# Cross-attention on one core: probabilities loaded back a slot later, keys stored in three planes

## The chip, the cores and the metric

The kernel runs on one core of a Trainium2 chip, alone. The metric is the time of one execution on the device in microseconds; the median of several runs counts. The engines are TensorE (PE, its weight loads shown as PEld), VectorE (DVE), ScalarE (ACT), GpSimd (POOL) and SyncE (SP), which here only issues DMAs.

## The reference

The input x is [32, 512, 640] float32, the context [32, 77, 1024], the weights are [640, 640] for queries and output and [1024, 640] for keys and values. There are 20 heads of 32 columns. The other slices of the context (objects, others, image prompt) are empty, so that one attention is left:

```
q = heads(x @ wq);  k = heads(ctx @ wk);  v = heads(ctx @ wv)     # 20 heads of 32
p = softmax(q k^T / sqrt(32))                                     # 512 x 77 per head
out = merge(p v) @ wo + bo + x
```

All products are made from float32 numbers split into a high and a low part: a product is three matmuls, high by high, high by low and low by high (`PAIRS`).

## The kernel before, in words

**Layout.** The 640 columns are five chunks j of 128 columns, four heads each. A *slot* n is one batch b and one chunk j (n = 5b + j, 160 slots). The keys and values of all 2464 context rows (five groups g of 512 rows, the last of 416) are computed in a prologue, split, and stored to scratch in HBM (`k_dram`, `v_dram`). The main loop loads them back per batch.

**Prologue.** For each group, `keys` and `values_of` make the products on TensorE, `split_keys` splits a key tile into high and low in a `ks` tile (two buffers) and issues its stores: three DMAs per tile, by GpSimd for all groups but the last, by SyncE for the last. The value products of the last group (`context_values(LAST, j, psv)`) are left for later: two before slot 0, one in slot 0 and two in slot 1 (`beside`).

**A slot.** In slot n TensorE makes the scores of chunk n in four parts (`scores`, L477), the queries of chunk n+1 in two parts (`queries`, L442), the attention values of an earlier chunk (`values`, L569), and two *pieces* of an output projection (`piece`, `project`, L612) of an earlier batch. ScalarE does the exponentials (`exps`, L495); GpSimd normalizes the chunk before (`normalize`, L510). `transpose_p(n - 1)` then transposes 32 x 32 blocks on DVE (z, L517) and stores the probabilities to HBM with four DMAs (pd, L524). `load_p` reads them back in another layout with two DMAs (raw, L533 and L534). A slot later the chunk is *taken*: `cast_p` (ACT, pp, L541), `rest_p` (ACT L547 and DVE L548) and `last_p` (POOL, L555) split it, `values` multiplies it, `sum_a`, `high_a` and `low_a` (L580 to L594) make the tile `at` that the projection reads.

**Lags.** `LAG = 3`: slot n takes chunk n-3, whose load was issued in slot n-1. Seen from the slot that loads: slot n calls `load_p(n - LAG + 1)`, which is chunk n-2, and the store of chunk n-2 stands late in slot n-1 (`transpose_p`). The ten pieces of a batch's projection are spread over the slots by `PIECES[j]` (batches back, first piece), the residual loads (xr, L601) and bias additions (POOL, L605) by `RESIDUAL` and `BIAS`.

**Output banks.** A projection half of 128 rows accumulates in one of two PSUM tiles `po`. `finish()` adds a completed half to its residual row block on DVE (L641), which frees the bank, and stores the rows (L647). Where `finish()` is called decides where that addition stands in DVE's order.

**Keys and values per batch.** Chunks 0 and 1 form group 0, chunks 2 to 4 group 1 (`GROUPS`). For each group there are two key tiles: `kb`, with the 308 columns of four heads for the high part of the query, and `kc`, with two halves of 154 columns for the other two products. `load_keys` issues two DMAs per head (L420, L423); `load_values` issues eight DMAs per group (L431). `refill` calls them in two halves per slot.

**Order.** The order of every engine is the order in which the program calls it; each engine runs its own list in order and waits on semaphores. SyncE issues all the DMAs of the main loop. A DMA on it also waits until the one issued eight before it has landed, since the completion semaphores are eight (DMAHW0 to DMAHW7) and are used in turn.

Of the kernel before, what the change touches and what calls it, by code (L numbers as in the profile page):

```python
# [51 lines left out]
def kernel(  # L52
# [41 lines left out]

    k_dram = dram.tile([P, NC_, 2, NT], FPR, name="k_dram")

    v_dram = dram.tile([NT + KPAD - NKEY, HPC, NC_, 3, HD], FPR, name="v_dram")
    wo_dram = dram.tile([P, NC_, 2, C], FPR, name="wo_dram")  # L100
# [106 lines left out]
    def split_keys(g, j):  # L207
        g0, gn = GROUPS_KV[g]
        ks = kvt.tile([P, 2, G], FPR, tag="ks", name="ks")
        split(ks[:, 0, :gn], ks[:, 1, :gn], pks.pop(j)[:, :gn])  # L210
        engine = nc.gpsimd if g + 1 < len(GROUPS_KV) else nc.sync
        dst = k_dram.rearrange("(h r) c w n -> r c w h n", h=2)[:, j, :, :, g0 : g0 + gn]
        engine.dma_start(dst[:, 0].bitcast(F32), ks[:64, :, :gn].bitcast(F32))
        for half in range(2):
            engine.dma_start(dst[:, 1, half].bitcast(F32), ks[64:, 1 - half, :gn].bitcast(F32))

    def values_of(g, j, pool):

# [176 lines left out]
    nc.sync.dma_start(bias, bo.unsqueeze(0).to_broadcast([P, C]))  # L395
    kbs, vbs, pnb = [], [], []
    for g, (j0, nj) in enumerate(GROUPS):
        kb = main.tile([P, nj, KCOLS], FPR, name=f"kb{g}")
        kc = main.tile([P, nj, 2, KCOLS // 2], FPR, name=f"kc{g}")
        for tile_ in (kb, kc):  # L400
            nc.gpsimd.memset(tile_.bitcast(F32), 0.0)
        kbs.append((kb, kc))
    for n in range(2):
        pn = main.tile([P, NQ * HPC, KPAD], F32, name=f"pn{n}")
        nc.gpsimd.memset(pn, 0.0)
# [7 lines left out]

    def load_keys(b, g, heads=range(HPC)):
        j0, nj = GROUPS[g]
        kb, kc = kbs[g]
        src = k_dram[:, j0 : j0 + nj, :, b * NKEY : (b + 1) * NKEY].bitcast(F32)
        for i in heads:
            r, half = slice(i * HD, (i + 1) * HD), i % 2 * NKEY
            nc.sync.dma_start(  # L420
                kb[r, :, i * NKEY : (i + 1) * NKEY].bitcast(F32), src[r, :, i // 2, :]
            )
            nc.sync.dma_start(kc[r, :, :, half : half + NKEY].bitcast(F32), src[r])  # L423

    def load_values(b, g, segments=SEGMENTS):
        j0, nj = GROUPS[g]
        v = v_dram.rearrange("n i j a d -> n j i (a d)")
        for p, t, r0, i, k0, kn in segments:
            k0 += b * NKEY
            c0 = i % 2 * HD  # L430
            nc.sync.dma_start(  # L431
                vbs[g][r0 : r0 + kn, :, p, t, c0 : c0 + 3 * HD].bitcast(F32),
                v[k0 : k0 + kn, j0 : j0 + nj, i, :].bitcast(F32),
            )
# [28 lines left out]
    def scores(n, t):  # L463
        b, j = divmod(n, NC_)
        g = GROUP_OF[j]
        qt, (kb, kc) = qts[n % 2], kbs[g]
        jg = j - GROUPS[g][0]
        sc = ps.tile([P, S], F32, tag="sc", name="sc", bufs=3)
        half = KCOLS // 2
        for m, (cols, keys_) in enumerate(  # L470
            (
                (slice(0, KCOLS), kb[:, jg]),
                (slice(0, half), kc[:, jg, 0]),
                (slice(half, KCOLS), kc[:, jg, 1]),
            )
        ):
            nc.tensor.matmul(  # L477
                sc[:, cols],
                qt[:, m, t * P : (t + 1) * P],
                keys_,  # L480
                start=(m == 0),
                stop=(m == 2),
            )
        nm = main.tile([P, HPC], F32, tag="nm", name="nm", bufs=3)
        nc.vector.tensor_reduce(  # L485
            nm, sc[:, :KCOLS].rearrange("p (h k) -> p h k", k=NKEY), AX.X, ALU.max, negate=True
        )
        return sc, nm
# [138 lines left out]
    def piece(b, i):  # L627
        for t, h, j in STEPS[CUTS[i] : CUTS[i + 1]]:
            if j == 0:
                output_bank(b, t, h)  # L630
            project(b, t, h, j)
            if j == NC_ - 1:
                closed.append((b, t, h))
# [12 lines left out]
            elif h == 1:  # L646
                nc.sync.dma_start(out[b, t * P : (t + 1) * P, :], xr)  # L647

    LATE = 2
    LAG = 3  # L650

    takes = {n + LAG: n for n in range(N)}

    PIECES = {2: (1, 0), 3: (1, 2), 4: (1, 4), 0: (2, 6), 1: (2, 8)}
    RESIDUAL = {1: (1, 0), 2: (1, 1), 3: (1, 2), 4: (1, 3)}
    BIAS = {2: (1, 0), 3: (1, 1), 4: (1, 2), 0: (2, 3)}
    TRANSPOSE_X = {0: ((), (0,), ()), 1: ((1,), (2,), ()), 2: ((3,), (), ())}
    SPLIT_X = {2: ((0,), (1,)), 3: ((2, 3), (4,))}  # L660

    WO = {1: (0, 1, 2), 2: (3,), 3: (4,)}
    wos = []

    def take(m):
# [5 lines left out]
    def refill(b, j, part):  # L671

        heads = range(2 * part, 2 * part + 2)
        segments = SEGMENTS[4 * part : 4 * part + 4]
        if j == 0:
            load_keys(b, 1, heads)
        elif j == 1:
            load_values(b, 0, segments)
        elif j == 2 and b + 1 < B:
            load_keys(b + 1, 0, heads)  # L680
        elif j == 3:
            load_values(b, 1, segments)

    def slot(n, beside=()):
        b, j = divmod(n, NC_)
        ahead, more = n + 1 < N, b + 1 < B
        back, first = PIECES[j]
        bo_, has_out = b - back, b >= back
        xsplits = SPLIT_X.get(j, ((), ())) if more and n > LATE else ((), ())
        turns = TRANSPOSE_X.get(j, ((), (), ())) if more and b else ((), (), ())  # L690
        if b == 1 and j < 2:
            turns = (((), (), ()), ((0, 1), (2,), ()))[j]
# [7 lines left out]
        if n - 1 in takes:  # L700
            high_a(takes[n - 1])
        bias_now = j in BIAS and b >= BIAS[j][0]
        if bias_now and (j in (2, 3) or not ahead):
            add_bias(b - BIAS[j][0], BIAS[j][1])
        s = scores(n, 0)
        if taken is not None:
            rest_p(taken)
        rs = sums(n - 1) if n else None
# [7 lines left out]
        if ahead:  # L716
            queries(n + 1, 0, 2)
        s = scores(n, 1)
        if n - LAG + 1 in pds and n > LATE:
            load_p(n - LAG + 1)  # L720
        if filling:
            refill(b, j, 0)
# [16 lines left out]
        if not ahead:  # L739
            exps(n, 2, *s)  # L740
            piece(bo_, first)
            s = scores(n, 3)
        early = ahead and has_out and j in (0, 3)
        if early:
            piece(bo_, first)
            finish()
# [1 line left out]
            transpose_p(n - 1)  # L748
        if ahead:
            split_q(n + 1)  # L750
            if bias_now and j not in (2, 3):
                add_bias(b - BIAS[j][0], BIAS[j][1])
            exps(n, 2, *s)
        if n and not has_out:
# [40 lines left out]
    def end():  # L795


        last = B - 1
        load_p(N - 2)
        piece(last - 1, 6)  # L800
        finish()
        high_a(N - 4)
        cast_p(N - 3)
        low_a(N - 4)
        rest_p(N - 3)
        last_p(N - 3)
        add_bias(last - 1, 3)
        piece(last - 1, 7)
        finish()
        transpose_p(N - 1)  # L810
        load_p(N - 1)
        load_residual(last, 0)
        load_residual(last, 1)
        piece(last - 1, 8)
        take(N - 3)
        piece(last - 1, 9)
        cast_p(N - 2)
        rest_p(N - 2)
        last_p(N - 2)
        finish()  # L820
        spare = late[0].tile([P, 3, S], F32, tag="raw", name="xr", bufs=2)
        load_residual(last, 3, spare.rearrange("p k q -> p (k q)")[:, :C])
# [24 lines left out]
        for t in (0, 1, 3, 2):  # L847
            add_bias(last, t)
        begin(2, 0, 3)
        begin(0, 2, 4)  # L850
        begin(1, 2, 4)
        begin(2, 3, 4)
        begin(3, 0, 4)
        take(N - 1)
        begin(4, 0, 4)
        begin(5, 0, 4)

        def close(t):
            for h in range(2):
                project(last, t, h, 4)  # L860
                closed.append((last, t, h))
            finish()

        close(0)
        close(1)
        begin(6, 0, 4)
        close(2)
        begin(7, 0, 4)
        close(3)
# [6 lines left out]
        transpose_x(1, i)  # L876
    for c in range(2):
        split_x(1, c)
    context_values(LAST, 1, psv)
    slot(0, (2,))  # L880
    kva.release()
    lw = ctx.enter_context(tc.tile_pool(name="lw", bufs=1, reuse_waits="tile"))
    wos.append(lw.tile([P, NC_, 2, C], FPR, name="wo_s"))
    slot(1, (3, 4))
    psv.release()
    kvp.release()
    late.append(ctx.enter_context(tc.tile_pool(name="late", bufs=1, reuse_waits="tile")))
    late.append(
        ctx.enter_context(tc.tile_pool(name="psl", bufs=1, space=PSUM, reuse_waits="tile"))
    )  # L890
    load_p(0)
    for n in range(LATE, N):
        slot(n)
    end()
# [40 lines left out]
```

## Time and profile before

| | |
|---|---|
| median of 3 runs | 2062.11 us (2056.33 to 2064.13) |
| profiled execution | 2062.03 us, span 2060.2 us |
| granted TensorE clock, mean | 0.976 |
| exponentials (ACT, L495) | 802.2 us, 2560 of 334 ns |
| projection (PE, L612) | 648.7 us, 3840 |
| queries (PE, L442) | 627.8 us, 2400 |
| values (PE, L569) | 275.9 us, 960 |
| normalizing (POOL, L510) | 364.4 us, 160 of 2277 ns |
| transposing probabilities (DVE, L517) | 241.9 us, 160 of 1512 ns |
| stores of probabilities (L524) | 640 DMAs of 160 KB, 3.5 us to landing |
| loads of probabilities (L533, L534) | 160 of 512 KB, 4.1 us; 160 of 128 KB, 4.2 us |
| loads of x (L253) | 128 of 320 KB, 7.2 us |
| DMA moved | 437.69 MB, 212 GB/s |

How to read it: the span runs from the first instruction to the last; an engine's busy time is the union of its instructions. Matmuls are pipelined, so the busy times of single groups overlap. A bracket at the end of a line of the timeline is the idle time of the engine before this instruction and what ended it. In the lists of waits the three numbers are the total in us, how many waits, and the longest. A window's line has the busy time of PE, PEld, DVE, ACT and POOL with the number of instructions, then the granted clock, the DMA engines' share of busy time and GB/s.

### The profile page before, as it was taken

To read this page: it belongs to the slowest core of one execution; us is meant where nothing else is said; L and a number is where in the kernel's file an instruction comes from. 1 tells how busy PE (TensorE), PEld (TensorE's weight loads), DVE (VectorE), ACT (ScalarE), POOL (GpSimd) and SP (SyncE) were. 2 spreads that over 40 slices of the span, in tenths; PEclk is the share of its full clock that TensorE was granted. 3 is DMA by queue.
4 is the path that set the end of the run, shared out by engine and by line. 5 is a ranking of instruction groups with operands and counts; after the bars stand their busy time and mean duration, and the time that the engine had idled before them with its cause. 6 is when DMAs were issued, how large, how long until landed. Compare 5 with 4: busy or idle time off the path is not lost.

```text
span 2060.2 us, 37687 instructions
## 1 busy us (share of the span) xinstructions
PE 1924.0 (93%) x10332; PEld 1686.9 (82%) x10332; DVE 1601.8 (78%) x2494; ACT 1538.7 (75%) x6210; POOL 1289.8 (63%) x1030
## 2 busy tenths in 40 slices
PE   9999997999999999999999999999999998999998
PEld 7777886888888888888888888887888787888887
DVE  4444437888888888888888888888888888888885
ACT  3232237888888888888888888888888787888893
POOL 1211165677766777777767766677677676777774
PEclk9999999999999999999999999999999999999999
DMA  9878878888888888889888888888888878888875
GB/s 184 187 176 228 187 181 203 215 228 220 214 214 221 222 224 223 222 222 229 221 210 219 220 218 210 225 221 206 214 216 226 203 210 212 230 220 217 217 205 175
DMA packets 586305, 437.69 MB, mean 212 GB/s; under 512 B 212400, under 2 KB 494448, under 8 KB 586096
## 3 DMA queue, kind: packets, MB, share of 16 engines
q1 hardware_dynamic: 580944, 420.78, 82.3%
q0 software_dynamic: 5056, 14.34, 2.6%
q8 instruction: 85, 1.39, 0.3%
q14 instruction: 124, 1.02, 0.1%
q10 hardware_dynamic: 96, 0.16, 0.0%
HBM read 253.48 MB, written 181.64 MB: 211 GB/s over the span
## 4 chain that ended last, share of the span: by engine, by line
ACT 25%; DVE 24%; DMA 17%; PE 8%; issue 4%; SPq 4%; POOL 3%; DVEq 0%; POOLq 0%; ACTq 0%
ACT pn L495 12%; DMA pd<-z 8%; DVE pp L548 7%; DMA raw<-pd 6%; DVE z L517 4%; ACT pp L541 4%; DVE nm L485 4%; ACT xt L264 3%; PE po L612 3%; ACT aw L580 3%; DVE at L594 3%; DVE qt L459 3%; SPq L524 2%; PE pq L442 2%; ACT qt L453 2%
## 5 line engine op out<-in xcount | busy, mean ns | idle before, releaser
L495 ACT ACTIVATE pn<-sc,nm 128x77 f32<-128x77 f32 x2560 | 802.2, 334 | 87.1 <-DVE nm L485 80.3
L612 PE MATMUL po<-wo_s,at 128*128 128x320 f32 x3840 | 648.7, 317 | 79.0 <-DVE xr L641 65.7
L612 PEld LDWEIGHTS po<-wo_s,at 128*128 128x128 f32 x3840 | 575.1, 191 | 92.5 <-DVE xr L641 74.0
L442 PE MATMUL pq<-xt,wq_s 128*128 128x512 f32 x2400 | 627.8, 401 | 4.3 <-POOL xt L265 2.2
L495 ACT ACTIVATION_READ_ACCUMULATOR pn<-sc,nm 128x1 f32 x2560 | 543.4, 212 | 0.0
L442 PEld LDWEIGHTS pq<-xt,wq_s 128*128 128x128 f32 x2400 | 429.3, 190 | 88.0 <-POOL xt L265 13.2
L555 POOL TENSOR_TENSOR pp<-raw,pp 64x512 fp32r<-64x512 f32 x160 | 236.5, 1478 | 318.2 <-ACT pp L547 296.4
L510 POOL TENSOR_TENSOR pn<-pn,rs 128x1232 f32<-128x1232 f32 x160 | 364.4, 2277 | 14.2 <-DVE rs L505 1.8
L605 POOL TENSOR_TENSOR xr<-xr,bias 128x640 f32<-128x640 f32 x128 | 229.0, 1790 | 159.8 <-DMA xr<-in_x_dram 109.4
L485 DVE TENSOR_REDUCE nm<-sc 128x4 f32<-128x308 f32 x640 | 291.4, 463 | 38.4 <-PE sc L477 33.8
L459 DVE TENSOR_TENSOR qt<-pq,qt 64x512 fp32r<-64x512 f32 x320 | 220.4, 689 | 117.7 <-ACT qt L453 112.6
L569 PE MATMUL pa<-pp,vb 128*128 128x512 f32 x960 | 275.9, 419 | 12.6 <-POOL pp L555 9.4
L548 DVE TENSOR_TENSOR pp<-raw,pp 128x1024 fp32r<-128x1024 f32 x160 | 232.7, 1454 | 66.0 <-ACT pp L541 65.5
L517 DVE STREAM_TRANSPOSE z<-pn 128x1280 f32<-128x1280 f32 x160 | 241.9, 1512 | 37.5 <-DMA pd<-z 17.0
L477 PEld LDWEIGHTS sc<-kc,qt 128*128 128x128 f32 x1280 | 216.1, 192 | 41.7 <-POOL qt L457 20.6
L477 PE MATMUL sc<-kc,qt 128*128 128x154 f32 x1280 | 231.3, 260 | 13.1 <-POOL qt L457 11.0
L541 ACT CAST pp<-raw 128x1024 fp32r<-128x1024 f32 x160 | 168.7, 1055 | 95.0 <-DMA raw<-pd 93.6
L582 DVE TENSOR_TENSOR pa<-pa,aw 64x512 f32<-64x512 f32 x320 | 222.6, 696 | 20.3 <-ACT aw L580 9.9
L569 PEld LDWEIGHTS pa<-pp,vb 128*128 128x128 f32 x960 | 181.0, 198 | 57.1 <-POOL pp L555 26.4
L265 POOL TENSOR_TENSOR xt<-xs,xt 128x512 fp32r<-128x512 f32 x160 | 205.3, 1304 | 34.8 <-ACT xt L264 28.5
L457 POOL CAST qt<-qt 64x512 fp32r<-64x512 f32 x320 | 195.7, 611 | 19.7
L477 PE MATMUL sc<-kb,qt 128*128 128x308 f32 x640 | 198.1, 310 | 9.5 <-DVE vs L104 4.7
(48 smaller groups left out, 1811.2 us busy)
## 6 DMA issues: line engine op xcount, KB each, us to landing
pd<-z SPq DMA_DIRECT2D x640, 160.0 KB, 3.5
raw<-pd SPq DMA_DIRECT2D x160, 512.0 KB, 4.1
xs<-in_x_dram SPq DMA_DIRECT2D x128, 320.0 KB, 7.2
xr<-in_x_dram SPq DMA_DIRECT2D x128, 320.0 KB, 3.9
out_dram<-xr SPq DMA_DIRECT2D x127, 320.0 KB, 4.0
raw<-pd SPq DMA_DIRECT2D x160, 128.0 KB, 4.2
v_dram<-vs SPq DMA_DIRECT2D x80, 192.0 KB, 4.0
kc<-k_dram SPq DMA_DIRECT2D x128, 57.8 KB, 3.3
```

The lines of the kernel that those rows point to most:

```text
L442: nc.tensor.matmul(pqs[n], wq_s[:, k, a, j * P : (j + 1) * P], xts[b, k][:, c, :], start=(k == 0 and m == 0), stop=(k == NC_ - 1 and m == 2),)
L459: nc.vector.tensor_tensor(qt[r, 1 + w, :], pq[r], qt[r, 0, :].bitcast(F32), ALU.subtract)
L477: nc.tensor.matmul(sc[:, cols], qt[:, m, t * P : (t + 1) * P], keys_, start=(m == 0), stop=(m == 2),)
L485: nc.vector.tensor_reduce(nm, sc[:, :KCOLS].rearrange("p (h k) -> p h k", k=NKEY), AX.X, ALU.max, negate=True)
L495: nc.scalar.activation(pnb[n % 2][:, at, :NKEY], sc[:, i * NKEY : (i + 1) * NKEY], AF.Exp, bias=nm[:, i : i + 1], accum_out=sms[n][:, at : ...
L510: nc.gpsimd.tensor_tensor(pf, pf, rs.unsqueeze(2).to_broadcast([P, NQ * HPC, NKEY]), ALU.mult)
L517: nc.vector.transpose(z.rearrange("p b t j -> p t b j"), pn.rearrange("p (t h) k -> p t (h k)", t=NQ).rearrange("p t (b i) -> p t b i", i=Q),)
L541: nc.scalar.copy(pp[:, 0:2, :], raw[:, 0:2, :])
L548: nc.vector.tensor_tensor(pp[:, 2:4, :], raw[:, 0:2, :], pp[:, 0:2, :].bitcast(F32), ALU.subtract)
L555: nc.gpsimd.tensor_tensor(pp[64:, 4, :], raw[:64, 2, :], pp[:64, 4, :].bitcast(F32), ALU.subtract)
L569: nc.tensor.matmul(pas[n][:, p, :], vb[:, p, t, :], pp[:, c, :], start=(c == p), stop=(t == 1),)
L612: nc.tensor.matmul(pos[b, t, h][:, :HALF], ats[b * NC_ + j][:, a, t * P : (t + 1) * P], wos[0][:, j, c, h * HALF : (h + 1) * HALF], start= ...
```

## The change

1. `LATE` becomes 3 and `LAG` 4. Slot n loads chunk n-3 and takes chunk n-4. The pieces of the projection, the residual loads and the bias additions move to the next slot; the early piece of a slot is now in j = 1 and 4 instead of 0 and 3. One `finish()` is added after the first scores of slots with j = 2.
2. The key scratch is two tensors, one for each group of chunks, with three planes each, so that one DMA per head brings what three places of the key tile need. `kb` and `kc` become one tile with four planes; the first score matmul reads planes 0 and 3. `split_keys` issues five DMAs per tile instead of three.
3. `refill` loads values of group 1 in slot j = 0 (of the batch before), keys of group 1 in j = 1, values of group 0 in j = 2, keys of group 0 for the next batch in j = 3. Before, these were keys of group 1, values of group 0, keys of group 0 and values of group 1, in the same four slots.
4. Of the value products of the last context group, one is left before slot 0; one is in slot 0, one in slot 1 and two in slot 2. The output weights are loaded in slots 4 to 6 instead of 1 to 3.
5. The end takes one chunk more and has two pieces more.

```diff
-    k_dram = dram.tile([P, NC_, 2, NT], FPR, name="k_dram")
+    k_dram = [dram.tile([P, 3, nj, NT], FPR, name=f"k_dram{j0}") for j0, nj in GROUPS]
...
         engine.dma_start(dst[:, 0].bitcast(F32), ks[:64, :, :gn].bitcast(F32))
+        engine.dma_start(dst[:, 1, 0].bitcast(F32), ks[:64, 0, :gn].bitcast(F32))
+        engine.dma_start(dst[:, 1, 1].bitcast(F32), ks[64:, 0, :gn].bitcast(F32))
         for half in range(2):
-            engine.dma_start(dst[:, 1, half].bitcast(F32), ks[64:, 1 - half, :gn].bitcast(F32))
+            engine.dma_start(dst[:, 2, half].bitcast(F32), ks[64:, 1 - half, :gn].bitcast(F32))
...
-        src = k_dram[:, j0 : j0 + nj, :, b * NKEY : (b + 1) * NKEY].bitcast(F32)
+        src = k_dram[g][:, :, :, b * NKEY : (b + 1) * NKEY].bitcast(F32)
         for i in heads:
             r, half = slice(i * HD, (i + 1) * HD), i % 2 * NKEY
             nc.sync.dma_start(
-                kb[r, :, i * NKEY : (i + 1) * NKEY].bitcast(F32), src[r, :, i // 2, :]
-            )
-            nc.sync.dma_start(kc[r, :, :, half : half + NKEY].bitcast(F32), src[r])
+                kbs[g][r, i // 2 : i // 2 + 3, :, half : half + NKEY].bitcast(F32), src[r]
+            )
...
-                (slice(0, KCOLS), kb[:, jg]),
-                (slice(0, half), kc[:, jg, 0]),
-                (slice(half, KCOLS), kc[:, jg, 1]),
+                (slice(0, KCOLS), kb[:, 0::3, jg]),
+                (slice(0, half), kb[:, 1, jg]),
+                (slice(half, KCOLS), kb[:, 2, jg]),
...
-    LATE = 2
-    LAG = 3
+    LATE = 3
+    LAG = 4
...
-    PIECES = {2: (1, 0), 3: (1, 2), 4: (1, 4), 0: (2, 6), 1: (2, 8)}
-    RESIDUAL = {1: (1, 0), 2: (1, 1), 3: (1, 2), 4: (1, 3)}
-    BIAS = {2: (1, 0), 3: (1, 1), 4: (1, 2), 0: (2, 3)}
+    PIECES = {3: (1, 0), 4: (1, 2), 0: (2, 4), 1: (2, 6), 2: (2, 8)}
+    RESIDUAL = {2: (1, 0), 3: (1, 1), 4: (1, 2), 0: (2, 3)}
+    BIAS = {3: (1, 0), 4: (1, 1), 0: (2, 2), 1: (2, 3)}
...
-    WO = {1: (0, 1, 2), 2: (3,), 3: (4,)}
+    WO = {4: (0,), 5: (1, 2), 6: (3, 4)}
...
-        if j == 0:
+        if j == 0 and b:
+            load_values(b - 1, 1, segments)
+        elif j == 1:
             load_keys(b, 1, heads)
-        elif j == 1:
+        elif j == 2:
             load_values(b, 0, segments)
-        elif j == 2 and b + 1 < B:
+        elif j == 3 and b + 1 < B:
             load_keys(b + 1, 0, heads)
-        elif j == 3:
-            load_values(b, 1, segments)
...
-        if bias_now and (j in (2, 3) or not ahead):
+        if bias_now and (j == 3 or not ahead):
             add_bias(b - BIAS[j][0], BIAS[j][1])
         s = scores(n, 0)
+        if j == 2:
+            finish()
...
-        if n - LAG + 1 in pds and n > LATE:
+        if n >= LATE:
             load_p(n - LAG + 1)
...
-        early = ahead and has_out and j in (0, 3)
+        early = ahead and has_out and j in (1, 4)
...
-    context_values(LAST, 1, psv)
-    slot(0, (2,))
+    slot(0, (1,))
+    slot(1, (2,))
+    slot(2, (3, 4))
...
-    slot(1, (3, 4))
...
-    load_p(0)
```

More of the change, by code (lines that the diff above doesn't have):

```diff
@@ L211, in split_keys @@
         engine = nc.gpsimd if g + 1 < len(GROUPS_KV) else nc.sync
-        dst = k_dram.rearrange("(h r) c w n -> r c w h n", h=2)[:, j, :, :, g0 : g0 + gn]
+        j0 = GROUPS[GROUP_OF[j]][0]
+        dst = k_dram[GROUP_OF[j]].rearrange("(h r) s c n -> r s h c n", h=2)[
+            :, :, :, j - j0, g0 : g0 + gn
+        ]
         engine.dma_start(dst[:, 0].bitcast(F32), ks[:64, :, :gn].bitcast(F32))
+        engine.dma_start(dst[:, 1, 0].bitcast(F32), ks[:64, 0, :gn].bitcast(F32))
+        engine.dma_start(dst[:, 1, 1].bitcast(F32), ks[64:, 0, :gn].bitcast(F32))
         for half in range(2):
-            engine.dma_start(dst[:, 1, half].bitcast(F32), ks[64:, 1 - half, :gn].bitcast(F32))
+            engine.dma_start(dst[:, 2, half].bitcast(F32), ks[64:, 1 - half, :gn].bitcast(F32))
     def values_of(g, j, pool):
@@ L397 @@
     for g, (j0, nj) in enumerate(GROUPS):
[L398 to L402, printed above, removed]
+        kb = main.tile([P, 4, nj, KCOLS // 2], FPR, name=f"kb{g}")
+        nc.gpsimd.memset(kb.bitcast(F32), 0.0)
+        kbs.append(kb)
     for n in range(2):
@@ L415, in load_keys @@
         j0, nj = GROUPS[g]
-        kb, kc = kbs[g]
-        src = k_dram[:, j0 : j0 + nj, :, b * NKEY : (b + 1) * NKEY].bitcast(F32)
+        src = k_dram[g][:, :, :, b * NKEY : (b + 1) * NKEY].bitcast(F32)
         for i in heads:
@@ L465, in scores @@
         g = GROUP_OF[j]
-        qt, (kb, kc) = qts[n % 2], kbs[g]
+        qt, kb = qts[n % 2], kbs[g]
         jg = j - GROUPS[g][0]
@@ L688, in slot @@
         bo_, has_out = b - back, b >= back
-        xsplits = SPLIT_X.get(j, ((), ())) if more and n > LATE else ((), ())
+        xsplits = SPLIT_X.get(j, ((), ())) if more and n > 2 else ((), ())
         turns = TRANSPOSE_X.get(j, ((), (), ())) if more and b else ((), (), ())
@@ L741, in slot @@
             piece(bo_, first)
+            finish()
             s = scores(n, 3)
-        early = ahead and has_out and j in (0, 3)
+        early = ahead and has_out and j in (1, 4)
         if early:
@@ L750, in slot @@
             split_q(n + 1)
-            if bias_now and j not in (2, 3):
+            if bias_now and j != 3:
                 add_bias(b - BIAS[j][0], BIAS[j][1])
@@ L798, in end @@
         last = B - 1
+        load_p(N - 3)
+        load_values(last, 1)
+        load_residual(last - 1, 3)
+        piece(last - 1, 4)
+        finish()
+        high_a(N - 5)
+        cast_p(N - 4)
+        low_a(N - 5)
+        rest_p(N - 4)
+        last_p(N - 4)
+        add_bias(last - 1, 2)
+        piece(last - 1, 5)
+        transpose_p(N - 1)
+        add_bias(last - 1, 3)
         load_p(N - 2)
@@ L801, in end @@
         finish()
-        high_a(N - 4)
+        take(N - 4)
+        piece(last - 1, 7)
         cast_p(N - 3)
-        low_a(N - 4)
         rest_p(N - 3)
         last_p(N - 3)
-        add_bias(last - 1, 3)
-        piece(last - 1, 7)
         finish()
-        transpose_p(N - 1)
         load_p(N - 1)
```

## The prediction

> **What bounds the kernel now.** I read the page first, for which engine is nearest to full.
>
> ```profile
> PE 1924.0 (93%) x10332; PEld 1686.9 (82%) x10332; DVE 1601.8 (78%) x2494; ACT 1538.7 (75%) x6210; POOL 1289.8 (63%) x1030
> ...
> PE   9999997999999999999999999999999998999998
> ...
> DMA  9878878888888888889888888888888878888875
> ```
>
> TensorE is nearly always busy, so time can come only from its holes and from what surrounds them. I cut the main part into slots in the timeline: a slot starts with the first group of six query matmuls (pq). An undisturbed slot lasts 9.83 us. Averaged by j over slots 9 to 156 they last 9.84 (j=0), 13.05 (j=1), 10.50, 10.74 and 10.16 us: 54.3 us per batch against 5 x 9.83 = 49.2. Of the 5.1 us lost, slot j=1 has 3.2. The windows of one bad batch (j=0 to 4; columns PE, PEld, DVE, ACT, POOL, clock, DMA share) show the same:
>
> ```profile
> 1586.80:1596.60 9.80, 9.80 (x59) 8.89 (x59) 8.54 (x15) 8.69 (x39) 6.50 (x6) 1.00 1.13 259
> 1596.60:1612.30 15.70, 11.48 (x60) 10.07 (x59) 10.45 (x16) 9.49 (x45) 5.73 (x5) 0.89 0.82 199
> 1612.30:1622.10 9.80, 9.80 (x60) 8.90 (x59) 9.27 (x17) 7.92 (x32) 7.11 (x6) 1.00 0.76 180
> ```
>
> Next the waits (engines, then SyncE's queue):
>
> ```profile
> ACT pp L541 <- DMA raw<-pd: 93.6, 33, 5.4
> PE po L612 <- DVE xr L641: 65.7, 30, 4.4
> ...
> ACT ks L103 <- DMA k_dram<-ks: 47.4, 12, 9.3
> ```
>
> ```profile
> SPq L533 <- DMA pd<-z: 123.4, 140, 3.6
> ```
>
> Thirty waits for an output bank are one per batch. The timeline of that j=1 slot shows where they come from:
>
> ```profile
> 1595.86 0.38 SPq L533 DMA_DIRECT2D raw<-pd  x1
> ...
> 1602.73 1.04 ACT L541 CAST pp<-raw 128x1024 fp32r<-128x1024 f32 x1 [5.10 <-DMA raw<-pd]
> ...
> 1603.81 1.23 DVE L548 TENSOR_TENSOR pp<-raw,pp 128x1024 fp32r<-128x1024 f32 x1 [3.76 <-ACT pp L541]
> ...
> 1606.04 0.48 DVE L641 TENSOR_TENSOR xr<-po,xr 128x320 f32<-128x320 f32 x1
> ...
> 1606.57 1.17 PE L612 MATMUL po<-wo_s,at 128*128 128x320 f32 x3 [4.22 <-DVE xr L641]
> ```
>
> The probability load is issued 9.1 us into slot 0, because SyncE waits for the store of the same probabilities to land. The cast in slot 1 waits for it, DVE's subtraction waits for the cast, the residual addition stands behind that subtraction in DVE's order, and TensorE waits for the bank which that addition frees. Slot 0 is the bad one because x of a later batch (4 loads of 320 KB) is fetched at the end of slot 4: the stores of slot 0 land after a median of 6.7 us (window of 1586.8 to 1596.6), those of slot 2 after 3.0.
>
> **The change, part by part.**
>
> *Load one slot later.* Slot n now loads chunk n-3, stored during slot n-2, so SyncE no longer waits for a fresh store (123.4 us over 140 slots, 0.9 each). I follow the queue in slot 0. The stores start about 1 us in and take 2.3 to 3.1 us to issue, four value loads 2.1, then the load: about 6 us in instead of 8 to 9.1. Landing takes 4.1 us (median) to 6.8 (in the bad batch), so it is there 10.1 to 12.8 us after slot 0 began; the cast is due at about 10.6. Slot 4 gains too: there the load waited for its store until 5 us in, with the x loads behind it; these now go about 2 us earlier, and slot 0 meets less of them. Left of the 3.2 us: 0 to 2, I take 0.8. That is -2.4 per batch.
>
> *An addition drawn forward.* In slot 2 the finish() after the first scores puts the residual addition ahead of the subtraction that waits for the cast. It costs nothing (0.47 us on DVE, the same number as before), covered by the same TensorE work; without the cover it is that 0.47. So even a late load would no longer hold the bank. I don't count this twice.
>
> *Projections, bias and residuals one slot later.* Per batch every engine does the same. The bias addition (1.79 us on POOL) leaves slot 2, where POOL waited at its start for a residual load, and where the windows of good batches show 11.3 us instead of 9.8: up to -1.4 per batch, but only in batches whose slot 1 was short. Slot 3 keeps a leading bias addition and three x subtractions (1.30 each). I take -0.5 for slot 2, nothing for 3 and 4.
>
> *Key loads.* 8 key issues per group (kb and kc, 0.3 to 0.6 us each) become 4 of three planes. Packets and bytes stay, so this saves about 1 us of SyncE's time, where it has slack. But the load of group 1 moves from slot 0 to slot 1 and is used by the first scores of slot 2: only one slot of margin. In slot 1: stores until 3.1, an output 0.4, two keys 1.0, probabilities 0.9, two keys 1.0: the last is issued at about 6. The nearest rows (kc of 57.8 KB, 3.3 us; kb 3.8) land it at 9.3 to 9.8; the scores are due at 9.3. Price: 0 to 0.5, up to 3 if it takes the 6.7 us of slot 0's stores; I take 0.5. The Trainium skill ("DMA: Bandwidth & Descriptors", "Anatomy of one DMA") fits 2.0 us + bytes/436 GB/s (for GpSimd's queue), an estimate of 2.2 us for 86.6 KB: by it no wait at all, and 15 us less in the sum. This trace's rows are above it.
>
> What a hole costs beyond itself is seen in another j=1 slot (timeline, then window):
>
> ```profile
> 1165.15 0.71 PE L612 MATMUL po<-wo_s,at 128*128 128x320 f32 x3 [2.43 <-DVE xr L641]
> ```
>
> ```profile
> 1157.00:1171.10 14.10, 11.67 (x60) 10.20 (x59) 10.70 (x17) 10.00 (x46) 5.71 (x5) 0.88 0.85 220
> ```
>
> A wait of 2.43 us lost 4.3, as the granted clock fell to 0.88 for the slot. The same skill ("TensorE: Matmul & The Clock Gate", "What's actually happening") has the clock fall after an idle window of some 3.4 us; by that rule holes of 2 us would cost only themselves. The row says otherwise, so I price holes over 2 us at 1.8 times their length.
>
> *Steady sum:* -2.4 - 0.5 + 0.5 = -2.4 per batch, 30 batches: -72 us.
>
> *Keys stored in three planes (prologue).* Five stores per tile instead of three; on POOL 0.52 us each (L215), 1.04 more per tile. The ks tile has two buffers and the cast waits for their landing (47.4 us in all), so the fifth cast of a group is 2 x 1.04 = 2.1 us later. TensorE waited for context behind this chain in two groups (4.89 and 1.03 us) and had 1.4 us to spare in the third: 2.1 + 2.1 + 0.7 = +4.9 us; 0 if other work hides it, 10 with the clock.
>
> *Last group and fill.* There the stores go by SyncE, 0.6 us each, ten more; through the two buffers this delays the last landing by about 3.9 us, and with it POOL's memset of vb (L411 waited 8.2 us for it), the query copy and the first scores (284.3). One context chunk (24 matmuls, 4.6 us) moves from before slot 0 into the fill. Slots 0 to 2 now hold four chunks instead of three: 34 us becomes 35, so slot 3 starts about 5 us later. +5 (0 to 9; below nothing no reason is seen).
>
> *Drain.* One more chunk's values (1.57) and 24 projection matmuls (two groups at 1.97) follow the last scores: 5.5 us, TensorE's work, with the dependent casts 6. In the fill they are missing, but slots 3 to 6 of before last 10.2 us with hardly a projection, so nothing is won there. +6 (5 to 9).
>
> **Sum.** 2062.0 (profiled execution; its span is 2060.2, the median of the runs 2062.1) - 72 + 4.9 + 5 + 6 = 2006.
>
> **Rivals.**
> 1. *The wait only shrinks:* slot 0's backlog of x stays and the load still lands at 12.8. Slot 1 keeps 2 us: -1.2 x 30 + 16 = -20, 2042. For it: DMA share of 1.13 in slot 0. Against: x starts earlier.
> 2. *All of it goes:* slot 1 clean and slot 2 too, -3.9 x 30 + 12 gives 1957. For it: slots of 9.83 are common. Against: slots 3 and 4 lose 1.2 us and run POOL and ACT full.
> 3. *Keys are late (slower):* if a group-1 load lands 6.7 us after issue, as slot 0's stores do, the first scores of slot 2 wait 3.4 us in every batch, 6 with the clock: (-2.9 + 6) x 30 + 16 = +109, 2171. It turns to a loss when slot 2 loses over 2.4 us per batch, a landing of about 5.3 us. For it: DMA share is 0.87 and rises to 0.9 with a shorter batch. Against: slot 1 comes after the backlog, where nothing in before waits for keys.
> 4. *No change:* gain eaten by fill, drain and a short key wait.
>
> **Chances.** My forecast 0.53, rival 1 0.16, rival 2 0.10, no change 0.07, rival 3 (any loss) 0.14. Runs of this kernel differ by 0.4%, so about 0.5% (10 us) is what can be told from none. Faster 0.79, same 0.07, slower 0.14. The range takes in rivals 1 and 2 and the upper end of the fixed costs: 1950 to 2055; it leaves out the loss and most of no change.
>
> **What would show it.** Right: SyncE's wait for pd at the load gone; ACT's wait for raw (93.6) under 30; TensorE's wait for xr (65.7) under 15; j=1 slots near 10.6; a few us more at slot 3 and in the end. Wrong: a wait of sc for key loads at j=2 slots (rival 3), j=1 slots still at 12 with ACT waiting for raw (rival 1), or a TensorE wait in the prologue above 15 us.

## The result and the profile after

The changed kernel takes 2128.5 us (median of 4 runs, 2125.2 to 2131.2) against 2059.2 before (2053.6 to 2064.1): 1.034 times as long (95% interval 1.030 to 1.037). The forecast was 2006, so it missed by 122.5 us, and the sign too. What happened is rival 3, late keys, which had a chance of 0.14.

The page of after: TensorE is busy for a smaller share of a longer span, and from slot 10 on every slice still shows nines, so the steady loss lies in short holes. (Rows: busy time; forty slices; the clock; the chain that ended last, by engine.)

```profile
PE 1941.3 (91%) x10332; PEld 1716.1 (81%) x10332; DVE 1581.1 (74%) x2494; ACT 1552.7 (73%) x6210; POOL 1268.1 (60%) x1068
...
PE   9898978799999999999999999999999999999998
...
PEclk9999989899999999999999999999999999999999
...
PE 56%; DMA 17%; DVE 8%; SPq 8%; ACT 6%; issue 3%; POOL 1%; DVEq 0%; ACTq 0%; POOLq 0%
```

The main part was cut into slots as in the prediction:

| stage | before | after |
|---|---|---|
| first slot starts at | 285.2 us | 303.5 us |
| slots 0 to 9 | 109.2 | 115.2 |
| slots 10 to 157 | 1606.5 | 1639.2 |
| last slots and end | 59.3 | 71.0 |
| mean slots j = 0 to 4 (10 to 155) | 9.84 13.11 10.52 10.72 10.17 | 9.83 14.13 11.53 9.84 10.10 |
| a batch | 54.36 | 55.42 |

The waits of TensorE, ScalarE and SyncE's queue in after:

```profile
PE sc L478 <- DMA kb<-k_dram: 99.0, 23, 15.4
PE sc L478 <- ACT pp L542: 29.8, 8, 4.6
...
PE po L613 <- DVE xr L642: 4.0, 2, 2.8
```

```profile
ACT pp L542 <- DMA raw<-pd: 84.1, 58, 3.2
...
ACT ks L103 <- DMA k_dram<-ks: 55.0, 12, 10.2
```

```profile
SPq L534 <- DMA pd<-z: 3.3, 6, 1.7
```

The wait for the output bank (65.7) is 4.0 and SyncE's wait for a fresh store (123.4) is 3.3: the two waits that the change was to remove are gone. In their place the first scores of slot j = 2 wait for group 1's keys in every batch: 99.0 us put down to the key load, of which 15.4 are the wait at the very first scores, and 29.8 more in 8 batches where the list names a cast (L542) as the last to come. In my cut this hole lies at the end of slot j = 1. The windows of slots j = 0 to 2 of one batch, and SyncE's timeline in slots 0 and 1 (start, time to issue), and TensorE's timeline where the first scores come:

```profile
1637.20:1647.00 9.80, 9.80 (x60) 8.89 (x58) 7.73 (x14) 8.86 (x40) 6.75 (x6) 1.00 1.01 261
1647.00:1660.70 13.70, 10.05 (x59) 8.90 (x58) 12.72 (x20) 10.04 (x41) 6.43 (x5) 1.00 0.90 232
1660.70:1672.10 11.40, 11.40 (x59) 10.19 (x59) 7.57 (x12) 8.09 (x34) 7.62 (x6) 0.85 0.61 174
```

```profile
1645.50 2.03 SPq L432 DMA_DIRECT2D vb<-v_dram  x4
1647.58 0.43 SPq L602 DMA_DIRECT2D xr<-in_x_dram  x1
1648.11 2.45 SPq L525 DMA_DIRECT2D pd<-z  x4
1650.66 0.64 SPq L648 DMA_DIRECT2D out_dram<-xr  x1
1651.40 1.77 SPq L422 DMA_DIRECT2D kb<-k_dram  x2
1653.27 0.56 SPq L534 DMA_DIRECT2D raw<-pd  x1
1653.88 0.48 SPq L535 DMA_DIRECT2D raw<-pd  x1
1654.41 2.11 SPq L422 DMA_DIRECT2D kb<-k_dram  x2
```

```profile
1660.32 0.56 PE L478 MATMUL sc<-kb,qt 128*128 128x308 f32 x3 [3.65 <-DMA kb<-k_dram]
```

Slot 1 begins at 1647.0. The last two key loads go out between 7.4 and 9.5 us into it, behind the probability load. Keys of such slots land 4.9 us after issue (median over all batches). The scores were due 9.7 us in and start at 13.3. The clock falls to 0.85 for the next slot, whose 9.8 us become 11.4. The fall is no gradual one: a window inside that slot shows half the clock, and the next one full speed again.

```profile
1661.00:1664.40 3.40, 3.40 (x11) 2.84 (x10) 3.12 (x7) 1.88 (x10) 2.54 (x2) 0.51 0.72 186
1664.40:1667.80 3.40, 3.40 (x20) 3.07 (x20) 1.83 (x4) 2.52 (x13) 2.68 (x3) 0.99 0.95 290
```

In the prologue TensorE waits longer for context (before first, then after):

```profile
PE pk L191 <- ACT ct L103: 10.1, 3, 4.9
```

```profile
PE pk L191 <- ACT ct L103: 18.2, 4, 7.8
```

### The profile page after: what moved, and what is told of

Same layout as the page of the kernel before. It is cut to its first block, busy times and chain, and to the rows that moved or that the text cites. A ratio compares the mean times of both kernels' runs of the same rounds, so it can differ in the third digit from the quotient of the medians.

```text
span 2129.0 us, 37333 instructions
## 1 busy us (share of the span) xinstructions
PE 1941.3 (91%) x10332; PEld 1716.1 (81%) x10332; DVE 1581.1 (74%) x2494; ACT 1552.7 (73%) x6210; POOL 1268.1 (60%) x1068
## 4 chain that ended last, share of the span: by engine, by line
PE 56%; DMA 17%; DVE 8%; SPq 8%; ACT 6%; issue 3%; POOL 1%; DVEq 0%; ACTq 0%; POOLq 0%
PE pq L443 21%; PE po L613 16%; PE sc L478 8%; PE pa L570 6%; DMA kb<-k_dram 5%; PE pk L191 5%; DMA raw<-pd 4%; SPq L422 2%; ACT pn L496 2%; DMA pd<-z 2%; DMA xs<-in_x_dram 2%; DMA k_dram<-ks 2%; DVE z L518 2%; SPq L525 2%; PE pv L191 1%
## 5 line engine op out<-in xcount | busy, mean ns | idle before, releaser
L443 PE MATMUL pq<-xt,wq_s 128*128 128x512 f32 x2400 | 665.5, 421 | 0.1
L613 PE MATMUL po<-wo_s,at 128*128 128x320 f32 x3840 | 639.1, 315 | 9.8 <-DVE xr L642 4.0
L443 PEld LDWEIGHTS pq<-xt,wq_s 128*128 128x128 f32 x2400 | 459.5, 203 | 85.0 <-POOL xt L270 0.5
L478 PEld LDWEIGHTS sc<-kb,qt 128*128 128x128 f32 x1920 | 339.8, 197 | 201.1 <-issue 112.7
L556 POOL TENSOR_TENSOR pp<-raw,pp 64x512 fp32r<-64x512 f32 x160 | 225.1, 1407 | 439.7 <-ACT pp L548 362.9
L478 PE MATMUL sc<-kb,qt 128*128 128x154 f32 (+1 forms) x1920 | 330.8, 282 | 146.4 <-DMA kb<-k_dram 99.0
L570 PE MATMUL pa<-pp,vb 128*128 128x512 f32 x960 | 253.3, 399 | 5.6 <-DMA vb<-v_dram 4.1
L549 DVE TENSOR_TENSOR pp<-raw,pp 128x1024 fp32r<-128x1024 f32 x160 | 212.1, 1325 | 28.5 <-ACT pp L542 28.5
L542 ACT CAST pp<-raw 128x1024 fp32r<-128x1024 f32 x160 | 168.6, 1054 | 84.2 <-DMA raw<-pd 84.1
L606 POOL TENSOR_TENSOR xr<-xr,bias 128x640 f32<-128x640 f32 x128 | 200.4, 1567 | 12.9 <-PE sc L478 2.9
L581 ACT COPY aw<-pa 64x1024 f32<-64x1024 f32 x160 | 162.0, 1013 | 59.7 <-PE pa L570 56.2
```

Of the source, the lines that this page charges most:

```text
L443: nc.tensor.matmul(pqs[n], wq_s[:, k, a, j * P : (j + 1) * P], xts[b, k][:, c, :], start=(k == 0 and m == 0), stop=(k == NC_ - 1 and m == 2),)
L478: nc.tensor.matmul(sc[:, cols], qt[:, m, t * P : (t + 1) * P], keys_, start=(m == 0), stop=(m == 2),)
L549: nc.vector.tensor_tensor(pp[:, 2:4, :], raw[:, 0:2, :], pp[:, 0:2, :].bitcast(F32), ALU.subtract)
L556: nc.gpsimd.tensor_tensor(pp[64:, 4, :], raw[:64, 2, :], pp[:64, 4, :].bitcast(F32), ALU.subtract)
L570: nc.tensor.matmul(pas[n][:, p, :], vb[:, p, t, :], pp[:, c, :], start=(c == p), stop=(t == 1),)
L613: nc.tensor.matmul(pos[b, t, h][:, :HALF], ats[b * NC_ + j][:, a, t * P : (t + 1) * P], wos[0][:, j, c, h * HALF : (h + 1) * HALF], start= ...
```

## Experiments

The questions: does the key load's place cost the steady loss; what does the new storage cost by itself; and what is left once both are mended. Ratios are to before in the same runs; "a batch" is the mean of slots 10 to 155 in the profiled execution.

**1. Keys in slot 0, beside the values.**

```diff
         if j == 0 and b:
+            load_keys(b, 1, heads)
             load_values(b - 1, 1, segments)
-        elif j == 1:
-            load_keys(b, 1, heads)
```

> The changed kernel with one edit: the keys of group 1 are loaded in slot j=0 beside the values of group 1, no longer in slot 1. Theory K (the keys have too little margin): TensorE's wait for the key tile at the first scores of slot 2 (3.7 us and the slower clock after it) goes; slot 1 falls from 14.1 to about 10.2 us, slot 2 from 11.5 to 9.9, 30 x 5.5 = 165 us less: about 1965. Rival Q (SyncE's queue and the DMA engines are full in slots 0 and 1, whoever is last waits): the four loads put into slot 0 push the probabilities or the values out by about 2 us, TensorE then waits for these in slot 1, and the time stays above 2080.

2051.5 us, 0.991 (0.988 to 0.994). A batch is 52.85 us: 9.83 10.44 10.56 10.59 11.43. The key hole is gone, as theory K has it, and slot 1 is 2.7 us shorter than before, the size that the forecast gave to the later probability load. Yet the time is 86 us above theory K's 1965: slots 1 and 2 stay 0.9 us longer than it expected, and slots 3 and 4 together are 2.1 us longer than in after. Waits for `at` are 1.2 of these 2.1:

```profile
PE po L613 <- DVE at L595: 36.7, 48, 1.4
```

**2. Keys in slot 0, values of group 1 in slot 4.**

```diff
+        if j == 0:
+            load_keys(b, 1, heads)
+        elif j == 4:
+            load_values(b, 1, segments)
...
-        load_values(last, 1)
```

> The changed kernel with the keys of group 1 in slot 0 and the values of group 1 in slot 4 instead of slot 0, so that slot 0 has four loads fewer than in e1. Theory K: as e1, about 1965, or 10 us less since slot 0 is lighter. Rival Q: the values now share slot 4 with the loads of x; the stores behind them are later, and the time stays above 2080.

2090.0 us, 1.010 (1.007 to 1.013), a batch 54.38, as rival Q has it: slot 1 is 12.31 again, with TensorE waiting for `at` before the values (39.8 us in 26 waits). The values now share slot 4 with the x loads, and in slot 0 the stores land in 7.2 us and the probabilities in 5.8 (6.7 and 4.0 in run 1). Slots 0 to 9 take 109.8 us instead of 115.7, so the longer start of the main part seems to come with loading the first batch's values in slot 5 rather than 4.

**3. The same with the key storage of before** (two planes, two DMAs per head, three stores).

```diff
-    k_dram = [dram.tile([P, 3, nj, NT], FPR, name=f"k_dram{j0}") for j0, nj in GROUPS]
+    k_dram = dram.tile([P, NC_, 2, NT], FPR, name="k_dram")
...
+            nc.sync.dma_start(kc[r, :, :, half : half + NKEY].bitcast(F32), src[r])
```

> e2 with the keys stored and loaded as before the change (two planes, two loads per head, 16 key loads per batch more): the later load of probabilities alone. If the three planes cost the 18 us that slot 0 starts later, slot 0 starts near 287 instead of 303.5 and the time is 15 us under e2; if it is the context product that was moved, slot 0 stays at 303 and the time is that of e2. If fewer key issues matter in the main loop (theory Q), e3 is slower there by 1 us per batch or more; by theory K the batches of e2 and e3 are alike within 0.3 us.

2078.3 us, 1.005 (1.003 to 1.008). The first slot starts at 282.6 us instead of 303.3; a batch is the same (54.35), though the profiled execution was the fastest of ten, 6.7 us below the median.

**4. Before, with the new key storage and nothing else.**

```diff
-    k_dram = dram.tile([P, NC_, 2, NT], FPR, name="k_dram")
+    k_dram = [dram.tile([P, 3, nj, NT], FPR, name=f"k_dram{j0}") for j0, nj in GROUPS]
```

> The kernel before with the new key storage alone: three planes, five stores per tile, one load per head, in the slots and with the lag of before. If the planes cost the prologue 15 us, slot 0 starts near 300 instead of 285. In the main loop slot 0 has four issues fewer, so the load of probabilities there is issued about 2 us earlier and slot 1 falls from 13 to about 11.5: -45 us. Sum about 2030. If issues don't matter: 2075.

2074.0 us, 1.002 (1.000 to 1.004): hardly a difference that this kernel's runs can tell, but two that nearly cancel. The first slot starts at 300.4 (+15.2 us); a batch is 53.82 (-0.54, about -16 us). The profiled execution was the fastest of ten, 11 us below the median, so a usual batch gains less, some 0.3 us (an estimate from the median: 15.2 less the 6.7 us by which it lies above before). Slot 1 fell to 12.64, not to the 11.5 expected. The end is 59.3 us, as before.

**5. The kernel of run 1 with the key storage of before.** The edit is that of run 3.

> e1 (2051.5 us) with the old key storage: two planes, three stores per tile, two loads per head, so that slot 0 issues eight key loads and eight value loads. If the planes cost the prologue 21 us, as slot 0 of e3 (282.6 against 303.3 in e2) says, slot 0 starts at 283. If the count of issues is what fills SyncE's queue, slot 0's load of probabilities is issued 2 us later than in e1 (8.4 us in) and slot 1 grows by 2 us, +60: about 2090. If packets and bytes are what counts, batches stay at 52.9 us and the time is about 2031.

2073.8 us, 1.007 (1.004 to 1.010). That is between the two expectations. First slot at 284.3 (-19.4), a batch 53.96 (+1.1 against run 1): with eight key issues in slot 0 its probability load goes out 8.9 us in instead of 8.4. So one key load per head does gain in this crowded slot, about half of the 2 us that the first expectation had.

**6. Run 1, with x of batches over 2 issued by GpSimd.**

```diff
-            nc.sync.dma_start(xs[q * Q : (q + 1) * Q, :, :], src[q])
+            (nc.gpsimd if b > 2 else nc.sync).dma_start(xs[q * Q : (q + 1) * Q, :, :], src[q])
```

> e1 with the loads of x issued by GpSimd from batch 3 on, everything else on SyncE. If the stores of slot 0 land late (6.7 us) because they stand behind x in the same queues, and the loads of x hold four of the eight semaphores in turn, then stores land in about 4 us, the load of slot 0 is issued 2 us earlier, and slots 1 and 2 go to 9.9: 30 x 1.2 = 35 us less, 2015. If it is the bytes of x that take the DMA engines, nothing moves by more than 0.3 us per slot and GpSimd's 4 x 0.5 us per batch cost up to 30 us.

2059.2 us, 0.999 (0.997 to 1.001), 44 us above the first expectation; a batch 53.11 (52.85 in run 1). In slot 0 the stores land in 4.0 us instead of 6.7 and the first of the two probability loads goes out 6.9 us in instead of 8.4, but it lands in 6.0 us instead of 4.0 and the keys in 6.5 instead of 4.5. The backlog moved from one transfer to the other.

**7. Run 1 with four stores per key tile, the same bytes** (the plane wanted twice is written by one DMA with a broadcast source).

```diff
+            if count > 1:
+                src = src.to_broadcast([64, count, gn])
+            engine.dma_start(dst[:, planes, h].bitcast(F32), src)
```

> e1 with the three planes filled by four stores per tile instead of five (two of them write one source into two planes), the same bytes written. If the prologue loses because a ninth DMA of GpSimd waits until the first has landed (two tiles of five stores are ten, 3.9 us waited at 109.0), then eight fit, that wait goes, each group gets 3 us or more back, and slot 0 starts near 292. If it is GpSimd's time to issue (0.52 us each), each group gets 1 us back and slot 0 starts near 300. If it is the bytes, it stays at 303.

2038.3 us, 0.989 (0.986 to 0.993). First slot at 292.4 instead of 303.7. The whole gains less against run 1 (0.991), since slots 0 to 157 take 5 us more here. Part of what one store less saves in the prologue is seen on GpSimd's queue (timeline, after first, then this run):

```profile
103.44 0.60 POOL L216 DMA_DIRECT2D k_dram<-ks  x1
104.03 0.52 POOL L217 DMA_DIRECT2D k_dram<-ks  x1
104.54 0.52 POOL L218 DMA_DIRECT2D k_dram<-ks  x1
109.01 1.04 POOL L220 DMA_DIRECT2D k_dram<-ks  x2 [3.94 <-DMA k_dram<-ks]
```

```profile
98.21 4.55 POOL L226 DMA_DIRECT2D k_dram<-ks  x8 [20.79 <-ACT ks L103]
```

The five stores of the first tile stand ahead of after's rows. Its queue stops for 3.94 us at the ninth store, until the first has landed; with four stores a pair of tiles is eight, and all go out at once. Such a stop comes twice in after, 6.3 us in all, and never here. Of the 11.3 us saved, 6.8 are there when the queries of chunk 0 start (278.3 in run 1, 271.5 here); the other 4.5 come between there and slot 0, behind the last group, whose stores SyncE issues. The run does not part the stops from the issues that are saved.

**8. After, with all four key loads in the first half of slot 1**, ahead of the probability load. Nothing else differs from after.

```diff
         elif j == 1:
-            load_keys(b, 1, heads)
+            if part == 0:
+                load_keys(b, 1)
```

> The changed kernel with the four key loads of group 1 still in slot 1, but all four in its first half, ahead of the load of probabilities. If the keys are late by their place in SyncE's queue, the last of them is issued about 2 us earlier (probabilities 1.1, and the half-slot order), the wait at slot 2 falls from 3.7 to about 1.7 us and the clock stays up: 30 x 3 = 90 us less, 2040. If it is the landing (a busy DMA, 4.9 us), the wait falls by less than 0.7 us: above 2100.

2034.5 us, 0.988 (0.985 to 0.992). A batch is 52.45: 9.83 11.16 10.03 10.29 11.15. The last key goes out 7.1 us into slot 1 (median; 8.2 in after), keys land in 3.4 us (4.9), and what is left of the hole (15.3 of the 34.7 us are the first scores) seldom pulls the clock down: it is 0.985 over the slot after it (0.845 in after), which lasts 10.03 us. The keys' landing in slot 1 of the same batch, after first, then this run:

```profile
kb<-k_dram SPq DMA_DIRECT2D x4, 86.6 KB, 4.5
```

```profile
kb<-k_dram SPq DMA_DIRECT2D x4, 86.6 KB, 3.2
```

Waits of TensorE and SyncE's timeline in that slot 1 of this run:

```profile
PE sc L478 <- DMA kb<-k_dram: 34.7, 18, 15.3
PE po L613 <- DVE at L595: 25.9, 35, 1.0
```

```profile
1582.82 3.11 SPq L422 DMA_DIRECT2D kb<-k_dram  x4
1586.03 0.55 SPq L534 DMA_DIRECT2D raw<-pd  x1
```

Two key loads moved ahead of the probability load; a batch got 3.0 us shorter, the profiled execution 92 us.

**9. Run 8, with the output products of slot 4 at their later place.**

```diff
-        early = ahead and has_out and j in (1, 4)
+        early = ahead and has_out and j == 1
```

> The run with the keys first in slot 1, with one more edit: the output products of a slot 4 are no longer put ahead of the split of the next queries, but after it, as in slots 0, 2 and 3 of that kernel. Theory: in that run a slot 4 takes 11.15 us where before it took 10.17, because its first output product waits for the remainder half of the attention output (at, written by the vector engine in the same slot; 35 waits of 0.4 to 1.0 us), and that wait is a cost of the longer lag which the prediction has not. Then slot 4 falls to 10.2 to 10.4 and the whole to 2034 - 30 x 0.85 = about 2008 (2003 to 2018). Rival: slot 4 is long because of what its transfers and conversions ask for (x loads in both halves); then the wait moves to the next user and slot 4 stays near 11, the whole at 2030 to 2040.

2190.8 us, 1.062 (1.057 to 1.066): the expectation was wrong by 183 us, and the rival's too. Slot 4 is 17.3 us; a window over one, and TensorE's timeline in it:

```profile
1499.00:1516.10 17.10, 13.07 (x59) 11.39 (x59) 11.07 (x16) 11.91 (x49) 12.04 (x9) 0.80 1.03 220
```

```profile
1504.45 0.86 PE L613 MATMUL po<-wo_s,at 128*128 128x320 f32 x4 [0.41 <-DVE at L595]
...
1510.53 5.17 PE L613 MATMUL po<-wo_s,at 128*128 128x320 f32 x18 [3.49 <-DVE xr L642]
```

So the early place matters: with it TensorE does not wait for an output bank in slot 4, presumably since VectorE can then free both banks before the second piece asks for one. The wait of 0.4 us that I wanted to remove stayed, and a hole of 3.49 came behind it. The slot is 7.3 us longer than 9.8: 3.9 us of holes, and 3.4 us lost at the clock of 0.80 (17.1 x 0.20).

**10. Run 9 with four stores.** The edits are those of runs 7 and 9.

> The same, with four key stores for each tile of keys instead of five, the bytes unchanged. By the run with four stores alone, the first slot starts some 11 us earlier and nothing else changes: about 1997 (1990 to 2007), 11 us under the run with the late output products of slot 4 alone. If the stores' gain is eaten by the first probability loads (whose slots 0 to 10 were up to 3 us longer in that run), it is 1 to 8 us.

2183.8 us, 1.059 (1.055 to 1.063), far from the 1997 expected, as run 9 was. The first slot starts 7.1 us earlier than in run 9 (291.5); the rest repeats run 9.

**11. Run 8 with four stores.** The edits are those of runs 7 and 8.

> The keys first in slot 1 and four key stores for each tile, both in one kernel: the two gains lie in different stages and should add. First slot starts at about 290 instead of 301; batches as with the keys first alone, 52.45; the whole at 2034 - 11 = about 2023 (2016 to 2032). If the two compete (stores are only in the prologue, so nothing should), it stays at 2034.

2027.0 us, 0.981 (0.978 to 0.984). First slot at 293.6 instead of 301.3; a batch 52.36. The gains add, 8 us instead of 11 from the stores.

**12. Run 11, with the rounding of `at` ahead of that of the probabilities in slot 4.**

```diff
+        if j == 4 and n - 1 in takes:
+            high_a(takes[n - 1])
         if taken is not None:
             cast_p(taken)
...
+        if j == 4 and n - 1 in takes:
+            low_a(takes[n - 1])
         if taken is not None:
             rest_p(taken)
```

> The same, with one more edit: in a slot 4, the scalar engine rounds the attention output (at) before it rounds the probabilities, and the vector engine makes the remainder of at before the remainder of the probabilities, not behind it. Theory: a slot 4 takes 11.15 us in the run with the keys first because its first output product waits 0.4 to 0.9 us for that remainder, a wait of the longer lag; by the vector engine's rows the remainder then ends about 1.5 us earlier and the probabilities' halves about 0.6 later, where a later user has several us. Slot 4 falls to 10.2 to 10.5, a batch by 0.6 to 0.9, the whole by 20 to 30 to about 2000. Rival: the slot is long for the conversions themselves (x, queries), and the wait moves to the next user: 2018 to 2026, or it grows as in the run that put the products later, where the output banks became the wait.

2025.4 us, 0.981 (0.977 to 0.985): nothing gained on run 11. The wait did go: slot 4 is 10.57 us instead of 11.27, and the output products' waits for `at` fell from 28.9 to 3.8 us. But slot 1 is 11.72 instead of 10.99, with the key hole back (43.8 us without the first scores' 11.5, against 22.1 in run 11):

```profile
PE sc L484 <- DMA kb<-k_dram: 55.3, 31, 11.5
...
PE po L619 <- DVE at L601: 3.8, 9, 1.1
```

A batch is 52.36 in both. What slot 4 won, slot 1 lost. The likely reading is that a TensorE which comes sooner to slot 2 finds the keys as late as they were.

## Why the prediction was wrong

The profiled execution missed the forecast by 2130.7 - 2006 = 125 us. Of this 105 lie in the steady part (+33 measured, -72 forecast) and 20 in the fixed costs (18.3 + 6.0 + 11.8 = 36.1 measured, 15.9 forecast).

- **Key loads: the step that failed.** It had the last key issued at about 6 us into slot 1 and landing in 3.3 to 3.8, so 0 to 0.5 us late, and took 0.5. Measured are 3.8 us of hole a batch (113.4 us of waits over 30 batches) and 2.1 more at the lowered clock. In after the last key goes out 8.2 us in (median; 8.9 in the batch shown) and the keys of the slot land in 4.9. Of the 2.2 us in the issue, 1.1 lie ahead of the first key, where the stores and the output were slower, 0.8 in the three key issues ahead of the last, and 0.2 in the probability load. One DMA in place of two does not take one issue's time: 0.61 us (median) against 0.44 and 0.43 for the pair. The landing is longer by 1.1 to 1.6; with the keys ahead of the probability load of 512 KB it is 3.4 (run 8). Runs 8 and 1 both show the place in the queue to be the cause: 88 us by 3.0 a batch, or 76 by 2.6. The prediction priced the landing from whole-run medians of smaller loads, and did not ask how long a larger one takes in this slot.
- **Rival 3 was right in its mechanism.** Its price (3.4 us, 6 with the clock) was near: 3.65, and 5.3 with the clock, in the batch shown. The cause it named, a landing of 6.7 us, was not needed; the issue gave some two thirds of the lateness and the landing one third. Its chance of 0.14 was too low because the point from which it decides, a landing of 5.3 us, was counted from an issue at 6.
- **Load one slot later: right in size, not by the path drawn, so partly luck.** Slot 1 was to lose 2.4 us less; run 1 shows 2.7 less. But there the load of slot 0 goes out 8.4 us in (before 8.8, forecast 6), and in slot 1 ScalarE still waits for it 80.5 us in 29 batches (92.5 before). So an earlier load is hardly what gained in run 1. In after the load goes out 7.3 us in, and the wait in slot 1 is halved to 44.0 us; nearly all the rest of the 84.1 in the list is new, in slot 2. What did go is TensorE's wait for the output bank (65.7 to 4.0). Two steps can carry that, and no run parts them: the addition drawn forward, which I put at nothing and did not count, and the projections' move by one slot, which takes the need for that bank from slot 1 to slot 2, where the cast waits less (1.1 us against 2.7 in run 1, medians). The load's place still matters beyond a point: in run 2, with the cast 4.1 us late in slot 1, TensorE waits for `at` instead. The x loads do go out earlier, but the stores of slot 0 land in 6.7 us, against 6.9 before: the backlog did not shrink.
- **Slot 2, -0.5: right** where no hole disturbs it (10.03 in run 8 against 10.52).
- **Slots 3 and 4, nothing: wrong in another way.** Once the key hole is gone they take 0.6 (run 8) to 1.1 us (run 1) a batch more than before, and 1.5 to 2.1 more than in after, in good part by waits for `at`. Probably the hole in after gives the vector engine time to catch up. Runs 9 and 12 show that neither a later use nor an earlier `at` turns this into time. What sets the 52.4 us of a batch, 3.2 above five undisturbed slots, stays open.
- **Three planes and the fill: under-priced.** Forecast 4.9 + 5, measured 18.3 to the first slot and 6.0 in slots 0 to 9. The planes alone cost 15.2 (run 4) to 20.7 (runs 2 and 3). Up to the queries of chunk 0 after is 12.3 us late (279.2 against 266.9), where 4.9 were forecast. The forecast went by two of TensorE's waits for context behind the key tiles; before has three, after has four, and they grew by 8.1 us (10.1 to 18.2). The clock was lower too, 0.94 against 0.97 up to there. I counted the time to issue two more stores and not that the ninth store on GpSimd waits for the first to land, two stops of 6.3 us in all; run 7, without them and with one issue less per tile, gives 11 back. The same limit on SyncE stands in the text on the kernel before, and I did not apply it to GpSimd. With four stores the first slot still starts 8 us later than with two planes (292.4 against 284.3); that rest, of bytes or issues, no run parts. The sign named for it, a TensorE wait above 15 us in the prologue, came (15.43 at the first scores).
- **End: 6 forecast, 11.8 measured.** Every run with the longer lag has 69 to 72 us there, run 4 without it 59.3. The 5.5 us of added TensorE work were counted. The rest are longer holes (9.1 us against 6.2, with waits for `at` and `xr` of up to 2.8) and a lower clock, 0.90 over this stretch against 0.97.
- **The two rules of the Trainium skill.** The fit of "DMA: Bandwidth & Descriptors", "Anatomy of one DMA", an estimate of 2.2 us, is farther off than the rows that I took: loads of this size land in 3.4 (run 8) to 4.9 us (after) here. On "TensorE: Matmul & The Clock Gate" see the last section.

## What to carry to other kernels

Before moving a load, write out its queue in the slot it moves to, with the times of the new transfers and not of those they replace, and compare the landing with the first use: a margin of zero is a loss, since TensorE's hole of over 3 us cost 1.7 or 3.4 us more by the clock here. A load that TensorE needs at the start of the next slot belongs ahead of a larger one that it needs only in the middle of it. When stores are split into more DMAs, count how many are in flight on that queue; one more than it held cost a wait for a landing here (3.94 us), not an issue time.

## What the runs showed of the hardware

- GpSimd's queue held eight stores in flight in this program: the ninth waited 3.94 us in one group and 2.36 in the next, and with eight per pair of tiles there was no such stop.
- Where holes pull the clock down: over the main parts (400 to 1950 us) of all fourteen profiled executions, the clock in the 10 us after a TensorE hole was 1.00 for all 98 holes of 1.1 to 1.7 us, mixed (0.70 to 1.00) from 1.7 to 3.1 us, and below 0.87 for all of the 88 holes above that. (Shorter holes are left out; where the clock fell after one, in runs 9 and 10, a longer hole followed it.) The window of some 3.4 us in the Trainium skill ("TensorE: Matmul & The Clock Gate", "What's actually happening") thus marks about where the drop is certain; it also comes after shorter holes, as the 2.43 us in the prediction did.
- What the drop costs: in these main parts a lowered clock is always 0.50, for 3.41 us (68 times) or 6.83 us (54 times), and then 1.00 at once. So a hole with a drop costs its length and 1.7 or 3.4 us more. In after, slots 1 and 2 of a batch are 6.0 us longer than two undisturbed ones: 3.9 of holes and 2.1 of clock. The factor of 1.8 in the prediction fitted its one row (2.43 + 1.7 = 4.1 of the 4.3 lost), but it is an added piece, not a factor.
- Taking x to another queue changed which transfer waited, not how much: the stores' landing fell by 2.8 us in slot 0, and that of the probability and key loads rose by some 2.0 (run 6).
